# Two GCN layers with graph attention on one core: seeding products in PSUM, another form of the layer norm, another order of steps

## The chip, the cores and the metric

The kernel runs on one core of a Trainium2 chip. The metric is the time of one execution on the device, in microseconds (us). The engines are called as in the profile: PE (TensorE, matrix products), DVE (VectorE), ACT (ScalarE), POOL (GpSimd) and SP (SyncE, which here only issues DMAs).

## The reference

64 graphs of 256 nodes with 512 features pass through two layers, all in float32. The first is a three-layer graph convolution, the second an attention that is restricted to sums over neighbours; each is added to its input and normalized over the features.

```
def _gcn_layer(x, adj, W, b):
    return adj @ (x @ W) + b

# layer 0
h = relu(_gcn_layer(x, adj, W1, b1)); h = relu(_gcn_layer(h, adj, W2, b2))
x = layernorm(x + _gcn_layer(h, adj, W3, b3))
# layer 1
q, k = split(x @ Wqk);  v = x @ Wv
agg = adj @ (k * mask)
w = mask * sum(q * agg, axis=-1) / sqrt(512)
x = layernorm(x + softmax(w, axis=nodes)[:, :, None] * v)
```

layernorm is (x - mean)/sqrt(var + 1e-5), without a gain or an offset. x has the shape (64, 256, 512) and adj (64, 256, 256); the adjacency is symmetric in its pattern only, so it comes transposed as an input of its own.

## The kernel before, in words

**Tiling.** Two graphs make a pair, and there are 32 pairs. A pair's nodes are two blocks of 128 (on the partitions) and the features two halves of 256. An operation on such a quarter of both graphs is 128x512: one PSUM bank.

**Products by Strassen.** Every product of 2 x 2 blocks is done with seven block products in place of eight (Winograd's form). `seven` (line 104) runs them in the order P1, P7, P6, P2, P5, P4, P3 on three PSUM banks: x takes P1, and then P6, P5 and P3 are added onto it; v takes P7 and then P4; y takes P2. Between them the other engines take out intermediate results: t1 (P1), u (x after P6) and t7 (P7) are copied to an SBUF tile `tmp` by ACT (line 109), or, where a matrix is to be added ("plus"), by an add on DVE (line 111). The four blocks of the result are c11 = y + t1, c22 = x + t7, c21 = v + u and c12 = x. PSUM has 8 banks in one pool (line 41). [...]

**Block sums.** The sums and differences of blocks that Strassen needs are made by `unit` (line 61). It puts an operation on DVE if its name is in `ON_DVE` (line 35), and on POOL otherwise. Names are made of a stage and a sum: "c1T7" is sum T7 of the first support product, "h17" and "x5" are sums of the moving matrix, "a3" and "a7" sums of the adjacency, "b3" the addition of the bias b3 to x.

**Stages of one pair.** Each is a Python generator that issues one block product, or one small group of operations, and yields:
- F, `front` (line 407): support product c1 (X W1, line 290), aggregation h1 (adj times it with relu, line 331), c2, h2, and c3; `load_xT` of the next pair after c1, and `load_x` (line 81) after h2.
- S, `sums` (line 417): the block sums of the next pair's x, the four b3 additions to this pair's x, and the adjacency sums of the next pair.
- B, `back` (line 433): layer 3's aggregation with x as plus (line 367), statistics, `inv_std` (line 371), the layer norm's `apply` (line 459), 32x32 transposes of the normalized r into `tr` on DVE (line 488), and from `tr` by DMA through `via` in DRAM into x1T (lines 491 to 495). `apply` does two things for each of four 128x512 parts: ACT writes the masked and scaled copy xm from r (line 460), and then DVE normalizes r in place (line 462).
- G, `gather`: adj times xm, which gives agg's factor, kept in gt.
- M, `attention` (line 515): Z and I are block sums of x1T for a nested Strassen; then come 7 + 7 products for a and b, taken in turn, and 7 + 7 for c and d (line 546), whose weights stream through a ring of 7 buffers. c and d have as plus the sums of R that DVE makes at lines 580 to 584 between the two. `score` (line 563) multiplies with gt and sums.
- E, `finish` (line 594): softmax over the nodes, v times the weights plus r, layer norm, and the output DMA.

**Order.** In round i the generators run for different pairs: F and S for pair i, B, G and M for pair i-1, and E for pair i-2. `run` (line 633) takes them in the order of a string in which each letter is one step: START for round 0, ORDER for rounds 1 to 30, LAST for round 31, and END for the last layers of pair 31. The schedule is manual: each engine has the instructions of its queue in the order in which the steps issue them, and the framework adds only the semaphore waits. So a letter's place in the string sets the place of all its instructions on PE, DVE, ACT, POOL and SP.

**Buffers.** tmp has 5 buffers, the support blocks (`sup`) 9; r is read by the layer norm, by the transposes and by E of the next round; x and xm share one buffer by tag, and so do tr and gt, and x1T and R's second part.

Of the kernel before, what the change touches and what calls it, by code (L numbers as in the profile page):

```python
# [9 lines left out]
FP = mybir.dt.float32  # L10
AF = mybir.ActivationFunctionType
OP = mybir.AluOpType
AX = mybir.AxisListType

P = 128
# [5 lines left out]
def gcn_then_graph_attention(ctx: ExitStack, tc: tile.TileContext, xT, xN, adjT, mask, W1, b1, W2, b2, W3, b3,  # L21
# [9 lines left out]
    KEYS = ("T1", "T2", "T3", "T4")  # L31
    SUP = 9
    SBUFS = 6
    TMP = 5
    ON_DVE = ('a5', 'c2T5', 'c2T6', 'c3T6', 'c3T7', 'h13', 'h23', 'h27', 'x3', 'x5')

    const = ctx.enter_context(tc.tile_pool(name="const", bufs=1))
    pool = ctx.enter_context(tc.tile_pool(name="work", bufs=1))
    small = ctx.enter_context(tc.tile_pool(name="small", bufs=2))
    dram = ctx.enter_context(tc.tile_pool(name="dram", bufs=2, space=bass.MemoryType.DRAM))  # L40
    psum = ctx.enter_context(tc.tile_pool(name="psum", bufs=8, space=bass.MemoryType.PSUM))

    E = mybir.EngineType
    ctx.enter_context(tc.manual_schedule(engines={E.PE, E.DVE, E.Activation, E.Pool, E.SP}))

    def bank(shape=(P, G, N)):
        return psum.tile(list(shape), FP, name="ps", tag="ps")

    def tmp():
        return pool.tile([P, D], FP, name="tmp", bufs=TMP)  # L50
# [53 lines left out]
    def seven(mm, shape, c11, c12, c21, c22, plus=None):  # L104

        def out(ps, k):
            t = shaped(shape)
            if plus is None:
                nc.scalar.copy(t, ps)  # L109
            else:  # L110
                add(t, ps, plus[k])
            return t

        x = bank(shape)
        mm(1, x, True)
        t1 = out(x, 0)
        yield
        v = bank(shape)
        mm(7, v, True)
        yield  # L120
        mm(6, x, False)
        u = out(x, 1)
        yield
        y = bank(shape)
        mm(2, y, True)
        t7 = out(v, 2)
        c11(y, t1)
        yield
        mm(5, x, False)
        c22(x, t7)  # L130
        yield
        mm(4, v, False)
        c21(v, u)
        yield
        mm(3, x, False)
        c12(x)
        yield
# [25 lines left out]
    def warm(n):  # L163

        ps = bank((P, P))
        for _ in range(n):
            nc.tensor.matmul(ps, lhsT=ident, rhs=ident, start=True, stop=True)

    warm(10)
    wl = {}  # L170
    begin, end = load_w(W1, 1, True)
# [110 lines left out]
    def support(src, w, who, last=None):  # L282

        sup = lambda: pool.tile([P, G, HD], FP, name="sup", tag="sup", bufs=SUP)
        C = {k: sup() for k in (3, 1, 5, 7, 6)}

        def mm(n, ps, first):
            for g in range(G):
                for c in range(2):
                    nc.tensor.matmul(ps[:, g], lhsT=src[n][:, c, g], rhs=w[n][:, c],  # L290
                                     start=(first and g == 0 and c == 0), stop=(g == G - 1 and c == 1),
                                     skip_group_check=True)

        def c21(v, t):
            add(C[5], v, t)
            unit(who + "T7", C[7], C[3], C[5], OP.subtract)
            unit(who + "T6", C[6], C[7], C[1])

        def c12(x):
            C[2], C[4] = sup(), sup()  # L300
            nc.scalar.copy(C[2], x)  # L301
            unit(who + "T5", C[5], C[5], C[1], OP.subtract)
            sub(C[4], x, C[6])
        steps = seven(mm, (P, G, HD), lambda y, t: add(C[3], y, t), c12, c21, lambda v, t: add(C[1], v, t))
        for _ in range(2):
            next(steps)
            yield
        if last is not None:
            last()
        yield from steps  # L310
        return C

    def aggregate(C, aS, b, who):

        hT = [pool.tile([P, 2, G, N], FP, name="hT", tag="act", bufs=2) for _ in range(2)]
        src, first, rest, last = a_sums(blocks(hT), who)
        blk = blocks(hT)

        def relu(i, j, ps=None):
            o = blk(i, j)  # L320
            for c in range(2):
                nc.scalar.activation(o[:, c], (o if ps is None else ps)[:, c], AF.Relu, bias=b[:, 2 - 2 * j + c:3 - 2 * j + c])  # L322

        def block(i, j, a, t):
            add(blk(i, j), a, t)
            relu(i, j)

        def mm(n, ps, first):
            for c in range(2):
                for g in range(G):  # L330
                    nc.tensor.matmul(ps[:, c, g], lhsT=C[n][:, g, c * P:(c + 1) * P], rhs=aS[n][:, g],  # L331
                                     start=(first and c == 0 and g == 0), stop=(c == 1 and g == G - 1),
                                     skip_group_check=True)
        for k, _ in enumerate(seven(mm, (P, 2, G, P), lambda y, t: block(0, 0, y, t), lambda x: relu(0, 1, x),
                                    lambda v, t: block(1, 0, v, t), lambda v, t: block(1, 1, v, t))):
            if k == 5:
                first()
            if k == 6:
                rest()
            yield  # L340
        return src, last
# [29 lines left out]
    def inv_std(mvt, n=G):  # L371

        sd = small.tile([P, NH, n], FP, name="sd")
        nc.scalar.activation(sd, mvt[:, :, :, 1], AF.Sqrt, bias=eps)  # L374
        rs = small.tile([P, NH, n], FP, name="rs")
        nc.vector.reciprocal(rs, sd)  # L376
        nb = small.tile([P, NH, n], FP, name="nb")
        nc.vector.scalar_tensor_tensor(nb, mvt[:, :, :, 0], -1.0, rs, op0=OP.mult, op1=OP.mult)  # L378
        return rs, nb

    def softmax_rows(w, gs):

# [50 lines left out]
    def back(i, C, aS, x, mask_t, end, put):  # L433
# [13 lines left out]
        yield from adj_times(aS, C, lambda y, t: add(rb(0, 1), y, t), lambda x: block(rb(0, 0), x, xb(0, 0), 0),  # L447
                             lambda v, t: block(rb(1, 1), v, t, 1), lambda v, t: add(rb(1, 0), v, t),
                             plus=(xb(0, 1), xb(1, 1), xb(1, 0)))

        rs, nb = inv_std(mvt)
        yield
        mrs = small.tile([P, NH, G], FP, name="mrs")
        nc.vector.scalar_tensor_tensor(mrs, rs, ISCALE, mask_t, op0=OP.mult, op1=OP.mult)
        mnb = small.tile([P, NH, G], FP, name="mnb")
        nc.vector.scalar_tensor_tensor(mnb, nb, ISCALE, mask_t, op0=OP.mult, op1=OP.mult)
        xm = pool.tile([P, G, NH, D], FP, name="xm", tag="x", bufs=1)

        def apply(h, g):
            nc.scalar.activation(xm[:, g, h, :], r[:, g, h, :], AF.Identity, scale=mrs[:, h, g:g + 1],  # L460
                                 bias=mnb[:, h, g:g + 1])
            nc.vector.tensor_scalar(r[:, g, h, :], r[:, g, h, :], rs[:, h, g:g + 1], nb[:, h, g:g + 1],
                                    op0=OP.mult, op1=OP.add)
        hg = [(h, g) for h in range(NH) for g in range(G)]
        xmb = [[xm[:, :, h, j * HD:(j + 1) * HD] for j in range(2)] for h in range(2)]
        if end:
# [1 line left out]
            x1T = [pool.tile([P, 2, G, N], FP, name="x1T", tag="act", bufs=2) for _ in range(2)]  # L468
            x1b = lambda h, k: x1T[k][:, :, :, h * P:(h + 1) * P]
            for h, g in hg:  # L470
                apply(h, g)
            yield
            xS = t_sums(xmb)
            for h, g in hg:
# [6 lines left out]
        else:  # L481
# [1 line left out]
            x1T = pool.tile([P, P, NH, 2, 2, G], FP, name="x1T", bufs=1)  # L483
            x1b = lambda h, k: x1T[:, :, h, k].rearrange("p n c g -> p c g n")
            for h, g in hg:
                apply(h, g)
# [13 lines left out]
        gb = lambda h, j: gt[:, h, :, j * HD:(j + 1) * HD]  # L500

        def gather():
            steps = adj_times(aS, xS, lambda y, t: add(gb(0, 0), y, t), lambda x: nc.scalar.copy(gb(0, 1), x),
                              lambda v, t: add(gb(1, 0), v, t), lambda v, t: add(gb(1, 1), v, t))
# [10 lines left out]
    def attention(i, x1b, w, r, mask_t, put):  # L515
# [23 lines left out]
        def inner(q, R, more=None):  # L539
# [15 lines left out]
            return seven(mm, (P, len(outer), HD), lambda y, t: add(R[:, :, 0, 0], y, t), c12,  # L555
                         lambda v, t: add(R[:, :, 1, 0], v, t), lambda v, t: add(R[:, :, 1, 1], v, t), plus=plus)
        v = pool.tile([P, G, NH, D], FP, name="v", tag="v", bufs=1)
        flat = lambda R: R.rearrange("p g j f -> p g (j f)")
# [35 lines left out]
    def finish(i, prev, gs=range(G)):  # L594
# [20 lines left out]
        rs, nb = inv_std(mvt, n)  # L615
        yield
        for k, g in enumerate(gs):
            for h in range(NH):
# [2 lines left out]
                yield  # L621
            nc.sync.dma_start(out[i, :, g * NH * D:(g + 1) * NH * D].rearrange("p (h f) -> p h f", h=NH), v[:, g])

    ORDER = ("BBFEFFBEBFBFBFBFFFBEFFFFBFSFBBBFFFBBBFGFFGGFFGFEEGMFFGMMMEGMMSFFMEMMEMMEFESMMEEFFMSM"
             "SMMMFMMMMFFEMMMMMMMMSMMMMMMFSMMMSSMMSSM")
    START = ("FFFBFBBFFBFBBBBBFFFFFFBBBBBFBBBBBBBBBBBFFBBBBSBFFBSBFBBFFFBBFBBFBFSFBFFBBBBFBBSFFBSB"
             "BSFBSFFSBBBSBBBBBSFBBBBBSBSBB")
    LAST = ("FBBSEFBFEBBFFBFBFBFFBFFFFEBBFFBBFBFBEFEEGFEGGFFEGEFFMMGSFFGMMMMFEFMMMMEMMMMMMEMMMFMM"
            "GSMMMMEMMMMMMMMFMMMSSMMMFMSSSFMFFSFSFSM")
    END = ("BEBBBBBBEBBBBBBBBGMGMEMMBEGGEEMGEGEMMMMMMEMEEMEMMMMMMMMMMMGMMBMMMMMMMMMMXMMXXMMMXYXM"  # L630
           "XMYXYMYYMYXYMYXYBMYMMXXYYXM")

    def run(order, rest, **gens):
        res = {}
# [81 lines left out]
```

## Time and profile before

| | |
|---|---|
| median of three runs | 2762.42 us (2761.38 to 2765.03) |
| the profiled execution | 2765.32 us |
| its span | 2763.5 us |
| mean granted clock of PE | 0.996 |
| busy in the span | PE 98%, PE's weight loads 87%, DVE 78%, ACT 41%, POOL 46% |
| matmuls' records, all | 14290 |
| DMA moved | 403.71 MB, mean 146 GB/s |

The page gives for each group of instructions its line, engine, operation, and out<-in by the names of the program, the count, the busy time, the mean of one in ns, and the idle time of its engine before it with what ended it. In the timeline, a line is a run of like instructions: its start in us, its length, engine, line, operation, tiles and count, and in brackets the wait ahead of it and its releaser. PEld stands for weight loads, SPq for issues of SP's queue. The ends of matmuls are modelled, so a stage on PE is best measured from start to start.

### The profile page before, as it was taken

What the parts mean: (1) busy time and instruction counts of PE and PEld (TensorE: products, weight loads), DVE (VectorE), ACT (ScalarE), POOL (GpSimd) and SP (SyncE); (2) the same over time, 40 slices, a digit from 0 to 9 for tenths busy, and PEclk for the clock granted to TensorE, in tenths of its full rate; (3) what the DMA queues carried; (4) which work ended last, traced back from release to release, by engine and by line L of the source; (5) the groups of instructions that cost most, each with busy time, mean ns of one, the idle gap of its engine ahead of it and who ended that gap; (6) DMA issues with size and microseconds to landing.
All of it is one profiled execution on the core that took longest, in us unless ns stands there. A gap on an engine that the chain in (4) does not pass through costs nothing. (4 is left out here: it accounts for less than half of the span.)

```text
span 2763.5 us, 41007 instructions
## 1 busy us (share of the span) xinstructions
PE 2716.9 (98%) x14290; PEld 2401.7 (87%) x14290; DVE 2145.0 (78%) x3828; ACT 1133.1 (41%) x2050; POOL 1262.8 (46%) x966
## 2 busy tenths in 40 slices
PE   9999999999999999999999999999999999999996
PEld 8888888888888888888888888888888888888885
DVE  5778777877777777778777777877787877778777
ACT  3434344434344343443334443434433444434343
POOL 3535455444554354544445543445544455434442
PEclk9999999999999999999999999999999999999998
DMA  6534554344544445543455444455434554434553
GB/s 209 165 110 147 165 175 135 117 143 154 163 151 123 126 147 162 173 135 112 143 162 162 141 129 131 147 162 176 133 115 141 161 162 148 130 123 147 162 155 97
DMA packets 202233, 403.71 MB, mean 146 GB/s; under 512 B 24752, under 2 KB 61872, under 8 KB 193968
## 3 DMA queue, kind: packets, MB, share of 16 engines
q1 hardware_dynamic: 202032, 401.10, 46.5%
q8 instruction: 117, 1.92, 0.3%
q14 instruction: 84, 0.69, 0.1%
HBM read 328.54 MB, written 72.48 MB: 145 GB/s over the span
## 5 line engine op out<-in xcount | busy, mean ns | idle before, releaser
L109 ACT COPY tmp<-ps 128x512 f32<-128x512 f32 x768 | 431.3, 584 | 643.3 <-PE ps L290 257.1
L62 POOL TENSOR_TENSOR sup<-sup 128x512 f32<-128x512 f32 x160 | 218.1, 1372 | 565.9 <-DVE sup L53 409.2
L546 PE MATMUL ps<-ring,I 128*128 128x256 f32 x1792 | 433.0, 381 | 7.7 <-DVE tmp L53 3.0
L546 PEld LDWEIGHTS ps<-ring,I 128*128 128x128 f32 x1792 | 334.1, 190 | 66.3 <-DVE R L53 11.7
L290 PE MATMUL ps<-w_T,S 128*128 128x256 f32 x1536 | 351.0, 381 | 9.2 <-POOL S L62 7.6
L301 ACT COPY sup<-ps 128x512 f32<-128x512 f32 x96 | 56.2, 586 | 722.2 <-PE ps L290 722.2
L290 PEld LDWEIGHTS ps<-w_T,S 128*128 128x128 f32 x1536 | 286.7, 190 | 59.7 <-POOL S L62 20.5
L546 PE MATMUL ps<-ring,Z 128*128 128x256 f32 x1344 | 327.9, 380 | 1.1 <-ACT Z L524 1.1
L59 POOL TENSOR_TENSOR I<-Z 128x384 f32<-128x384 f32 (+1 forms) x128 | 190.1, 1504 | 244.5 <-DVE Z L527 150.8
L546 PEld LDWEIGHTS ps<-ring,Z 128*128 128x128 f32 x1344 | 254.4, 190 | 38.4 <-ACT Z L524 3.3
L331 PEld LDWEIGHTS ps<-aT,sup 128*128 128x128 f32 x2048 | 253.5, 192 | 13.2 <-issue 6.6
L331 PE MATMUL ps<-aT,sup 128*128 128x128 f32 x2048 | 261.8, 276 | 1.8
L53 DVE TENSOR_TENSOR R<-ps,tmp 128x512 f32<-128x512 f32 (+1 forms) x384 | 221.2, 616 | 48.7 <-PE ps L546 48.4
L62 POOL TENSOR_TENSOR x<-x,b3b 128x512 f32<-128x512 f32 x128 | 192.2, 1523 | 128.7 <-DMA x<-in_xN 119.3
L290 PE MATMUL ps<-w,hT 128*128 128x256 f32 x1024 | 242.0, 379 | 0.0
L290 PE MATMUL ps<-w_T,hT 128*128 128x256 f32 x1024 | 236.5, 379 | 0.0
L290 PEld LDWEIGHTS ps<-w_T,hT 128*128 128x128 f32 x1024 | 194.6, 190 | 26.5
L53 DVE TENSOR_TENSOR sup<-ps,tmp 128x512 f32<-128x512 f32 x288 | 192.8, 677 | 30.8 <-PE ps L290 30.7
L290 PEld LDWEIGHTS ps<-w,hT 128*128 128x128 f32 x1024 | 192.0, 190 | 24.7
L331 PE MATMUL ps<-aS,sup 128*128 128x128 f32 x1536 | 206.3, 279 | 1.7 <-ACT tmp L109 1.1
L322 ACT ACTIVATE hT<-hT,b 128x256 f32<-128x256 f32 x384 | 167.4, 501 | 87.1 <-DVE hT L53 86.2
L331 PEld LDWEIGHTS ps<-aS,sup 128*128 128x128 f32 x1536 | 188.9, 192 | 11.4 <-DVE hT L53 4.8
(116 smaller groups left out, 4762.8 us busy)
## 6 DMA issues: line engine op xcount, KB each, us to landing
ring<-mv SPq DMA_DIRECT2D x672, 256.0 KB, 3.6
x<-in_xN SPq DMA_DIRECT2D x32, 1024.0 KB, 8.0
out<-v SPq DMA_DIRECT2D x64, 512.0 KB, 7.6
xT<-in_xT SPq DMA_DIRECT2D x31, 1024.0 KB, 5.0
via<-tr SPq DMA_DIRECT2D x31, 1024.0 KB, 4.2
x1T<-via SPq DMA_DIRECT2D x124, 256.0 KB, 4.7
ring<-mv SPq DMA_DIRECT2D x224, 128.0 KB, 3.1
aT<-in_adjT SPq DMA_DIRECT2D x32, 512.0 KB, 3.9
```

Source lines behind the costliest of these rows:

```text
L53: nc.vector.tensor_tensor(o, a, b, op=OP.add)
L59: (nc.gpsimd).tensor_tensor(o, a, b, op=op)
L62: (nc.vector if name in ON_DVE else nc.gpsimd).tensor_tensor(o, a, b, op=op)
L109: nc.scalar.copy(t, ps)
L290: nc.tensor.matmul(ps[:, g], lhsT=src[n][:, c, g], rhs=w[n][:, c], start=(first and g == 0 and c == 0), stop=(g == G - 1 and c == 1), skip ...
L301: nc.scalar.copy(C[2], x)
L322: nc.scalar.activation(o[:, c], (o if ps is None else ps)[:, c], AF.Relu, bias=b[:, 2 - 2 * j + c:3 - 2 * j + c])
L331: nc.tensor.matmul(ps[:, c, g], lhsT=C[n][:, g, c * P:(c + 1) * P], rhs=aS[n][:, g], start=(first and c == 0 and g == 0), stop=(c == 1 and ...
L546: nc.tensor.matmul(ps[:, k], lhsT=left[n](place[o]), rhs=wt[:, k], start=(first and k == 0), stop=(k == len(outer) - 1), skip_group_check= ...
```

## The change

What it does, in parts:

1. *Seeds.* In `seven`, P1's result is copied by ACT (or added to its plus by DVE) straight into the bank y, in PSUM, instead of into an SBUF tmp. P2 is then accumulated onto it with `start` false. c11 therefore is y alone: an ACT copy to its place, or in `aggregate` a relu that reads y, in place of a DVE add of y and t1. y comes from a pool of its own of two banks; the other pool has six. At the start of the program 16 small matmuls with an identity write both seed banks.
2. *Layer norm of layer 0.* `turn`, on DVE and first, is (r - mean)*rs in place. `masked`, on ACT and after it, is xm = r*ms, with ms = mask/sqrt(512). Before it was ACT first, from the raw r with a scale and an offset, and then DVE. The small tiles nb, mrs and mnb go in `back` (nb stays in `finish`); ms is new.
3. *Engines of the sums.* `ON_DVE` gains a3, a6, a7, b3, c1T5, c1T6, c1T7, c2T7, h17, h25 and h26, and loses c3T6, h13, x3 and x5.
4. *Order.* All four strings are new.

```diff
-    ON_DVE = ('a5', 'c2T5', 'c2T6', 'c3T6', 'c3T7', 'h13', 'h23', 'h27', 'x3', 'x5')
+    SEEDS = 2
+    ON_DVE = ('a3', 'a5', 'a6', 'a7', 'b3', 'c1T5', 'c1T6', 'c1T7', 'c2T5', 'c2T6', 'c2T7', 'c3T7', 'h17', 'h23', 'h25', 'h26', 'h27')
-    psum = ctx.enter_context(tc.tile_pool(name="psum", bufs=8, space=bass.MemoryType.PSUM))
+    psum = ctx.enter_context(tc.tile_pool(name="psum", bufs=8 - SEEDS, space=bass.MemoryType.PSUM))
+    def seed_bank(shape=(P, G, N)):
+        return psum.tile(list(shape), FP, name="seed", tag="seed", bufs=SEEDS)
...
         x = bank(shape)
         mm(1, x, True)
-        t1 = out(x, 0)
+        y = seed_bank(shape)
+        if plus is None:
+            nc.scalar.copy(y, x)
+        else:
+            add(y, x, plus[0])
         yield
...
-        y = bank(shape)
-        mm(2, y, True)
+        mm(2, y, False)
         t7 = out(v, 2)
-        c11(y, t1)
+        c11(y)
...
+    seeds = [seed_bank((P, 4, P)) for _ in range(SEEDS)]
+    for t in seeds:
+        for k in range(4):
+            nc.tensor.matmul(t[:, k], lhsT=ident, rhs=ident, start=(k == 0), stop=(k == 3), skip_group_check=True)
     warm(10)
...
-        steps = seven(mm, (P, G, HD), lambda y, t: add(C[3], y, t), c12, c21, lambda v, t: add(C[1], v, t))
+        steps = seven(mm, (P, G, HD), lambda y: nc.scalar.copy(C[3], y), c12, c21, lambda v, t: add(C[1], v, t))
...
-        for k, _ in enumerate(seven(mm, (P, 2, G, P), lambda y, t: block(0, 0, y, t), lambda x: relu(0, 1, x),
+        for k, _ in enumerate(seven(mm, (P, 2, G, P), lambda y: relu(0, 0, y), lambda x: relu(0, 1, x),
...
-        rs, nb = inv_std(mvt)
-        yield
-        mrs = small.tile([P, NH, G], FP, name="mrs")
-        nc.vector.scalar_tensor_tensor(mrs, rs, ISCALE, mask_t, op0=OP.mult, op1=OP.mult)
-        mnb = small.tile([P, NH, G], FP, name="mnb")
-        nc.vector.scalar_tensor_tensor(mnb, nb, ISCALE, mask_t, op0=OP.mult, op1=OP.mult)
+        ms = small.tile([P, NH, G], FP, name="ms")
+        nc.vector.tensor_scalar(ms, mask_t, ISCALE, None, op0=OP.mult)
+        rs = inv_std(mvt)
+        yield
...
-        def apply(h, g):
-            nc.scalar.activation(xm[:, g, h, :], r[:, g, h, :], AF.Identity, scale=mrs[:, h, g:g + 1],
-                                 bias=mnb[:, h, g:g + 1])
-            nc.vector.tensor_scalar(r[:, g, h, :], r[:, g, h, :], rs[:, h, g:g + 1], nb[:, h, g:g + 1],
-                                    op0=OP.mult, op1=OP.add)
+        def turn(h, g):
+            nc.vector.tensor_scalar(r[:, g, h, :], r[:, g, h, :], mvt[:, h, g, 0:1], rs[:, h, g:g + 1],
+                                    op0=OP.subtract, op1=OP.mult)
+
+        def masked(h, g):
+            nc.scalar.activation(xm[:, g, h, :], r[:, g, h, :], AF.Identity, scale=ms[:, h, g:g + 1])
...
-    ORDER = ("BBFEFFBEBFBFBFBFFFBEFFFFBFSFBBBFFFBBBFGFFGGFFGFEEGMFFGMMMEGMMSFFMEMMEMMEFESMMEEFFMSM"
-             "SMMMFMMMMFFEMMMMMMMMSMMMMMMFSMMMSSMMSSM")
+    ORDER = ("BBFEFFBBEFBBFBFBFFFFFBFFFFBFBBBFFFBFSEBGGFSGGEFEEGFMSGMFMGMFMFMFMMMEMMFMFMMMSMFEEESM"
+             "SMEMFEFSEFMMMFMSMMMMSMMMMMMMMSMMMMSMMMF")
```

The products c11 of `back` (layer 3), of G and of M change in the same way as that of `support`: each add of y and t becomes an ACT copy of y. In ORDER, counted by letters: c3's last product moves to the very end of the round; the steps of S come at letters 36 to 118 in place of 26 to 121, the x sums (36, 42, 52) ahead of most of M; of b3's four steps (76, 82, 84, 91) three stand ahead of the sums of R (lines 580 to 584; letters 85, 87 and 94), and in before two (82, 84; sums at 87, 89, 90), there on POOL. The first part of the layer norm is issued after P2 of h1 (before: after P4), the second after P1 of c2, the third and fourth after P7 of c2 (before: three after P1 of c2).

More of the change, by code (lines that the diff above doesn't have):

```diff
@@ L376, in inv_std @@
         nc.vector.reciprocal(rs, sd)
-        nb = small.tile([P, NH, n], FP, name="nb")
-        nc.vector.scalar_tensor_tensor(nb, mvt[:, :, :, 0], -1.0, rs, op0=OP.mult, op1=OP.mult)
-        return rs, nb
+        return rs
     def softmax_rows(w, gs):
@@ L446, in block @@
                     nc.vector.bn_aggr(mvt[:, h, g], st[:, h, g])
-        yield from adj_times(aS, C, lambda y, t: add(rb(0, 1), y, t), lambda x: block(rb(0, 0), x, xb(0, 0), 0),
+        yield from adj_times(aS, C, lambda y: nc.scalar.copy(rb(0, 1), y), lambda x: block(rb(0, 0), x, xb(0, 0), 0),
                              lambda v, t: block(rb(1, 1), v, t, 1), lambda v, t: add(rb(1, 0), v, t),
                              plus=(xb(0, 1), xb(1, 1), xb(1, 0)))
-        rs, nb = inv_std(mvt)
+        ms = small.tile([P, NH, G], FP, name="ms")
+        nc.vector.tensor_scalar(ms, mask_t, ISCALE, None, op0=OP.mult)
+        rs = inv_std(mvt)
         yield
-        mrs = small.tile([P, NH, G], FP, name="mrs")
-        nc.vector.scalar_tensor_tensor(mrs, rs, ISCALE, mask_t, op0=OP.mult, op1=OP.mult)
-        mnb = small.tile([P, NH, G], FP, name="mnb")
-        nc.vector.scalar_tensor_tensor(mnb, nb, ISCALE, mask_t, op0=OP.mult, op1=OP.mult)
         xm = pool.tile([P, G, NH, D], FP, name="xm", tag="x", bufs=1)
-        def apply(h, g):
-            nc.scalar.activation(xm[:, g, h, :], r[:, g, h, :], AF.Identity, scale=mrs[:, h, g:g + 1],
-                                 bias=mnb[:, h, g:g + 1])
-            nc.vector.tensor_scalar(r[:, g, h, :], r[:, g, h, :], rs[:, h, g:g + 1], nb[:, h, g:g + 1],
-                                    op0=OP.mult, op1=OP.add)
+        def turn(h, g):
[3 more added lines that the diff above has]
+            nc.scalar.activation(xm[:, g, h, :], r[:, g, h, :], AF.Identity, scale=ms[:, h, g:g + 1])
         hg = [(h, g) for h in range(NH) for g in range(G)]
@@ L470, in back @@
             for h, g in hg:
-                apply(h, g)
+                turn(h, g)
+                masked(h, g)
             yield
@@ L485, in back @@
             for h, g in hg:
-                apply(h, g)
+                turn(h, g)
+                masked(h, g)
                 for k in range(2):
@@ L502, in gather @@
         def gather():
-            steps = adj_times(aS, xS, lambda y, t: add(gb(0, 0), y, t), lambda x: nc.scalar.copy(gb(0, 1), x),
+            steps = adj_times(aS, xS, lambda y: nc.scalar.copy(gb(0, 0), y), lambda x: nc.scalar.copy(gb(0, 1), x),
                               lambda v, t: add(gb(1, 0), v, t), lambda v, t: add(gb(1, 1), v, t))
@@ L554, in inner @@
                 plus = (more[:, :, 0, 0], more[:, :, 1, 0], more[:, :, 1, 1])
-            return seven(mm, (P, len(outer), HD), lambda y, t: add(R[:, :, 0, 0], y, t), c12,
+            return seven(mm, (P, len(outer), HD), lambda y: nc.scalar.copy(R[:, :, 0, 0], y), c12,
                          lambda v, t: add(R[:, :, 1, 0], v, t), lambda v, t: add(R[:, :, 1, 1], v, t), plus=plus)
@@ L614, in finish @@
                 nc.vector.bn_aggr(mvt[:, h, k], st[:, h, k])
-        rs, nb = inv_std(mvt, n)
+        rs = inv_std(mvt, n)
+        nb = small.tile([P, NH, n], FP, name="nb")
+        nc.vector.scalar_tensor_tensor(nb, mvt[:, :, :, 0], -1.0, rs, op0=OP.mult, op1=OP.mult)
         yield
@@ L622, in finish @@
             nc.sync.dma_start(out[i, :, g * NH * D:(g + 1) * NH * D].rearrange("p (h f) -> p h f", h=NH), v[:, g])
-    ORDER = ("BBFEFFBEBFBFBFBFFFBEFFFFBFSFBBBFFFBBBFGFFGGFFGFEEGMFFGMMMEGMMSFFMEMMEMMEFESMMEEFFMSM"
-             "SMMMFMMMMFFEMMMMMMMMSMMMMMMFSMMMSSMMSSM")
[L626 to L631, printed above, removed]
+    ORDER = ("BBFEFFBBEFBBFBFBFFFFFBFFFFBFBBBFFFBFSEBGGFSGGEFEEGFMSGMFMGMFMFMFMMMEMMFMFMMMSMFEEESM"
+             "SMEMFEFSEFMMMFMSMMMMSMMMMMMMMSMMMMSMMMF")
+    START = ("BBFFFFFBBFFBBBBBFFFFFFFBBBBBFSFBBBBSBBBFBBBBBFBBBBBBBFBBFFFFFFBSFFFFSBBBBBBFSFBFBSBS"
+             "BBFBBSFSSBSBBBBBBBBBBBFBBBSBB")
+    LAST = ("FFBEBFBBEBBFFBSFBFFFEFFBSFSFFBFBFFBBFBBEEFGEEEGFGGFGFMMFMGFMFMFGMFMEEMMMMFMFFMMMSSEM"
+            "SMSFMSEMMFSFMMMMMEMFMMMMMMMMMMFMMSMMMSM")
+    END = ("BBBBBBBBBBBEBBBBGGEMGGMEMBGEEEBGMMMMEMMMMEMEMMEEEBMMMMMMGMMMMMMMMMMMMMMMMXMMXXMMXYMX"
+           "YMYXMXMXYXYMMXMMYYYYXYYMXMY")
     def run(order, rest, **gens):
```

## The prediction

> **What bounds the kernel now.** I read part 1 of the page first, then the start of each round (one round is one pair) in the timeline, then one middle round, 1005.35 to 1090.76, line by line in the timeline, and last the groups by form and the waits.
>
> ```profile
> PE 2716.9 (98%) x14290; PEld 2401.7 (87%) x14290; DVE 2145.0 (78%) x3828; ACT 1133.1 (41%) x2050; POOL 1262.8 (46%) x966
> ```
>
> ```profile
> 76.75 1.89 PE L290 MATMUL ps<-w,xT 128*128 128x256 f32 x8
> 2523.56 1.89 PE L290 MATMUL ps<-w,xT 128*128 128x256 f32 x8
> ```
>
> TensorE is the bound. From the first product of c1 in one round to that in round 30 lie (2523.56 - 76.75)/29 = 84.37 us each. What PE must do in a round: the trace records two instructions for a matmul, issued 0.216 us apart for 256 columns (8 in 1.73) and 0.112 us for 128. A round has 322 x 0.216 = 69.5, 112 x 0.112 = 12.5 and some 0.4 of softmax: 82.4. So 84.37 - 82.4 = about 1.9 us of each round is PE standing still, and only that can be won. The other engines have slack: per round DVE 67, POOL 39.5, ACT 35.4 busy. What matters is where PE stands still. The timeline of the middle round:
>
> ```profile
> 1021.19 3.85 POOL L62 TENSOR_TENSOR sup<-sup 128x512 f32<-128x512 f32 x3 [12.48 <-DVE sup L53]
> 1022.42 1.05 PE L331 MATMUL ps<-aT,sup 128*128 128x128 f32 x8
> 1023.31 2.12 PE L331 MATMUL ps<-aS,sup 128*128 128x128 f32 x16
> 1025.27 3.14 PE L331 MATMUL ps<-aT,sup 128*128 128x128 f32 x24
> 1028.37 1.16 PE L331 MATMUL ps<-aS,sup 128*128 128x128 f32 x8
> 1029.36 1.89 PE L290 MATMUL ps<-w,hT 128*128 128x256 f32 x8
> 1030.15 1.27 POOL L62 TENSOR_TENSOR S<-hT 128x512 f32<-128x512 f32 x1 [5.12 <-ACT hT L322]
> 1031.48 3.72 PE L290 MATMUL ps<-w_T,S 128*128 128x256 f32 x16 [0.23 <-POOL S L62]
> 1031.87 2.23 ACT L460 ACTIVATE xm<-r,mnb,mrs 128x512 f32<-128x512 f32 x3
> 1032.72 1.65 DVE L462 TENSOR_SCALAR r<-r,rs,nb 128x512 f32<-128x512 f32 x1
> 1035.32 0.47 DVE L462 TENSOR_SCALAR r<-r,rs,nb 128x512 f32<-128x512 f32 x1
> 1036.74 0.47 DVE L462 TENSOR_SCALAR r<-r,rs,nb 128x512 f32<-128x512 f32 x1
> ```
>
> Three readings. First, h1 takes 1029.36 - 1022.42 = 6.94 for 56 products worth 6.27: 0.67 lost, behind POOL's three c1 operations T7, T6, T5 at 1.28 each. Second, c2 starts at 1029.36 and its P7 at 1031.48, 2.12 where 1.73 is due: with 0.11 behind it, 0.50 lost for h17, one POOL operation of 1.27. Third, the same in-place operation of line 462 costs 0.47, or 1.65 [...].
>
> ```profile
> 1071.99 5.68 POOL L62 TENSOR_TENSOR x<-x,b3b 128x512 f32<-128x512 f32 x3 [4.29 <-DMA x<-in_xN]
> 1081.15 1.46 PE L546 MATMUL ps<-ring,Z 128*128 128x256 f32 x6
> 1082.25 1.61 DVE L53 TENSOR_TENSOR tmp<-ps,R 128x512 f32<-128x512 f32 x3
> 1082.99 1.56 PE L546 MATMUL ps<-ring,I 128*128 128x256 f32 x6 [0.38 <-DVE tmp L53]
> 1084.39 1.46 PE L546 MATMUL ps<-ring,Z 128*128 128x256 f32 x6
> ```
>
> Fourth: in the c and d products PE waits for DVE's adds of "more" (tmp), 0.96 us in this round. Start of M: 0.59. Softmax: 0.24. Sum: 2.96. The next round loses only 1.45: c1/h1, h17 and softmax recur, the rest varies (mean of c/d about 0.4).
>
> ```profile
> L109 ACT COPY tmp<-ps 128x512 f32<-128x512 f32 x768 | 431.3, 584 | 643.3 <-PE ps L290 257.1 <-DVE r L53 152.4 <-PE ps L367 135.5
> L53 DVE TENSOR_TENSOR R<-ps,tmp 128x512 f32<-128x512 f32 x288 | 192.0, 683 | 48.7 <-PE ps L546 48.4
> L462 DVE TENSOR_SCALAR r<-r,rs,nb 128x512 f32<-128x512 f32 x128 | 109.8, 858 | 49.8 <-ACT xm L460 49.8
> ```
>
> [...]
>
> **The change part by part.** Each cost is per round.
>
> *Seeds.* A round has eleven runs of `seven`; three have a plus (layer 3's product, here L3, and c and d). DVE loses c11 where ACT copies now: c1, c2, c3, G, a, b are 6 x 0.68; h1 and h2 lose an add and relu reads PSUM, 2 x 0.68; L3, c and d lose 0.69 + 0.68 + 0.42. Together 7.2. ACT gains 9 copies of about 0.58, less in d: about 5. The seed itself is the old copy with another goal: [...] I take 0.584. PE's count stays; 16 matmuls at the start lie under the load of W1, which PE awaits until 9.5. Is there a new wait of PE? P2 now waits for the seed. But P6, which goes into the bank of P1, already waited for that same reader, and P2 comes after P6: no. Two banks of eight are set aside; each seven holds three at a time, and the seed bank turns over once in two sevens, 5 us or more for a reader of 0.6: nil. If that cover goes, it is one ACT copy, 0.6.
>
> *ON_DVE.* To DVE: a3, a6, a7, b3 (four), c1T5 to T7, c2T7, h17, h25, h26, at about 0.65 (0.35 for the a's): 8.9. To POOL: c3T6, h13, x3, x5 twice: -4. Layer norm loses small DVE operations, -0.45. DVE: 67 - 7.2 - 0.45 + 8.9 - 4 = about 64 of 84; ACT 40; POOL 28. No engine becomes the bound by its sum.
>
> *c1 to h1.* Three operations of 0.65 in place of 1.28 and c11 gone from DVE ahead of them: 0.67 falls to about 0.2. Next late is the ACT relu chain. Gain 0.47.
>
> *h17.* 0.66 for 1.27 (0.61 sooner), but it queues behind h1's last add on DVE: 0.50 to about 0.25. Gain 0.25.
>
> *c and d.* DVE loses 1.1 of c11 here and gets the four b3 adds. These wait for x (issued at the start of c3, landing 8.0 later by the table of DMA issues; the shortest I found was 6.9) and hold DVE's queue: the sum of R parts, 1.23 each, and the adds of "more" stand behind. From landing to P6 of c DVE needs 3 x 0.65 (b3) + 2 x 1.23 + 3 x 0.65 + 1.22 + 0.65 + 0.36, which ends some 0.3 to 0.6 before P6 of c is due. With that slack the stall goes from 0.4 to 0.05, gain 0.35. If x lands at its latest (8.8) [...], P6 of c is 0.4 to 1.0 late.
>
> *Layer norm.* In before ACT reads r first and DVE waits for it; now `turn` goes first, the transposes start 0.8 sooner, and `masked` waits for `turn`. Queued behind the masked ones on ACT is the copy of P6 of c2, for which P5 of c2 waits. From the end T of h17: turns start at T, T + 1.43 and T + 2.85 (cycle by the two last lines of line 462: 1036.74 - 1035.32 = 1.42, a turn and two transposes). Then 0.47 + 0.81 + 0.58 and semaphores: T + 4.8. P5 is due at T + 3 x 1.73 = T + 5.2: slack 0.35. POOL runs h16, h15, h13 at that time[...]. New wait, taken at 0; its ends are 0 and 2.0.
>
> *Order.* More DVE work beside POOL in G's third product and in h2: -0.15. Start of M, where the Z copies queue on ACT behind more copies: -0.1. Softmax keeps 0.24. Ends for both: 0 and twice that.
>
> Sum: 0.47 + 0.25 + 0.35 - 0.25 = 0.82 a round. 30 rounds: -25. The last layer norm, with nothing to hide it, hands r on about 1.3 sooner, and some finish work moves: -2. The profiled execution was 2765.3 (span 2763.5 and 1.8 around it), 2.9 above the median of 2762.4: 2765.3 - 27 = 2738, against the median 2736 to 2738; I say 2737, 0.9% faster.
>
> **The rivals.** *More gained:* all waits but softmax and 0.25 more go, as the next round with its 1.45 shows that c/d and M's start may be nil. 1.9 - 0.5 = 1.4 x 30 + 2 = 44: 2718. For it: DVE's load falls just where PE waited. Against it: the two new waits in the queues. *Given back:* x late [...], +0.8: 0.82 goes to 0, 2763. [...] *Slower:* [...] P5 of c2 waits 2.0 behind `masked` on ACT. In nine rounds of ten that is 1.8 on the mean: +1.8 - 0.82 = +1.0, x 30 less 2 = 28: 2790. In every round, with the adds of c 0.5 late as well, it would be +1.7 and 2811. It decides from where the fourth turn ends later than T + 3.65 by more than 0.8. [...] *Not what it says:* the seed adds no product and removes none, so if all stalls were set by DMA nothing would change; the three recurring stalls name POOL and DVE, so I leave it within the given-back case.
>
> **How the numbers follow.** Forecast 2737: 0.48. More gained, 2718: 0.18. Given back, 2763: 0.12. Slower, 2790: 0.22. What a measurement of this kernel can tell from no change is about 0.2%, 5.5 us; so faster 0.66, same 0.12, slower 0.22. Range: from 2714, just under the bigger gain (leaving under 0.05), to 2780, which cuts most of the slower case (0.15). Forecast and bigger gain have their own range, 2714 to 2750.
>
> **What would show it.** Right: rounds of 83.5 us from c1 to c1; h1 in under 6.5; P7 of c2 within 1.9 of its start; no PE wait at P6 of c; the tmp copies of line 109 down from 768 to 512 and 256 new ACT copies into the seed bank at some 0.58. Wrong: PE waits at line 290 for an ACT tmp in c2, turns of 1.65 more often than one in four, PE waiting for DVE's tmp at the first adds of c just behind x's landing, or seeds much over 0.66. The prediction is wrong altogether if a round is 84.4 or more.

## Result and profile after

The kernel after took 2727.74 us (median of four runs, 2725.27 to 2730.18), the kernel before 2763.73 in the same measurement (2761.38 to 2769.49). The ratio is 0.9864, with a 95% interval of 0.9846 to 0.9882: 36 us or 1.4% faster. The forecast was 2737. The direction held; 36 us were gained where the prediction had summed 27.

Page of after, part 1, the line that answers to the one shown of before:

```profile
PE 2694.6 (99%) x14306; PEld 2410.4 (89%) x14306; DVE 2118.6 (78%) x3700; ACT 1278.4 (47%) x2338; POOL 925.5 (34%) x678
```

PE has 16 more records and 99% of the span. These are the start-up matmuls with the identity: 8 of them (two banks by four), with two records each, so "16 matmuls" in the part on the change and in the prediction counts records. ACT took 145 us more, 4.5 a round (5 was the estimate), POOL 337 less. DVE has hardly less to do, 2119 for 2145.

Start of rounds 1 and 30, timeline of after:

```profile
78.21 1.89 PE L301 MATMUL ps<-w,xT 128*128 128x256 f32 x8
2487.96 1.89 PE L301 MATMUL ps<-w,xT 128*128 128x256 f32 x8
```

(2487.96 - 78.21)/29 = 83.09 us a round, where before had 84.37. Most rounds of after are 83.03 to the hundredth: 82.43 of products and 0.60 of standing still. The 1.28 per round are 37.1 us in 29 rounds. The work from the start of round 31 to the last product is 3.35 shorter, round 30 is 1.1 shorter, and the first round (round 0) ends 1.5 later: 40 us in all, the difference of the two spans (2763.5 and 2723.5). The medians lie 36 apart, since the profiled execution of after was the fastest of its four.

The seams around h1 and c2, timeline of after, one round that starts at 992.01 (line numbers of after: 342 is aggregation, 301 support, 467 `turn`, 471 `masked`, 113 the tmp copy):

```profile
1009.08 1.05 PE L342 MATMUL ps<-aT,sup 128*128 128x128 f32 x8
1015.69 1.89 PE L301 MATMUL ps<-w,hT 128*128 128x256 f32 x8
1016.44 0.69 DVE L66 TENSOR_TENSOR S<-hT 128x512 f32<-128x512 f32 x1 [0.97 <-ACT hT L333]
1017.42 3.62 PE L301 MATMUL ps<-w_T,S 128*128 128x256 f32 x16
1019.98 0.46 DVE L467 TENSOR_SCALAR r<-r,mvt,rs 128x512 f32<-128x512 f32 x1
1020.47 0.72 ACT L471 ACTIVATE xm<-r,ms 128x512 f32<-128x512 f32 x1 [0.70 <-DVE r L467]
1021.10 1.05 ACT L113 COPY tmp<-ps 128x512 f32<-128x512 f32 x2
```

h1 takes 1015.69 - 1009.08 = 6.61 (6.94 before, 6.27 due; the prediction's sign was under 6.5). P7 of c2 starts 1.73 after c2, with no wait, and h17 is done 0.3 before. The fourth turn costs 0.46. None of the 128 turns is longer than 0.6, where in before 31 of 128 took over 1.4. POOL was running beside all of those 31. But it also ran beside 62 turns of after, and beside the third turn of 31 rounds of before, and each of these took under 0.5: POOL at work does not by itself make the operation long here. `masked` waits 0.70 for it, and the copy of u for c2's P5 is behind `masked`, as foreseen; P5 doesn't wait.

The start of the c products, same round:

```profile
1055.14 1.90 DVE L66 TENSOR_TENSOR x<-x,b3b 128x512 f32<-128x512 f32 x3 [2.08 <-DMA x<-in_xN]
1062.81 1.02 DVE L57 TENSOR_TENSOR seed<-ps,R 128x512 f32<-128x512 f32 x2
1063.82 2.54 PE L556 MATMUL ps<-ring,I 128*128 128x256 f32 x11
```

DVE stands 2.08 us waiting for x with the b3 adds, and the seeds of c and d are there in time all the same: PE runs 11 instructions without a gap. One line more from the groups by form, and one from the page's table of DMA issues:

```profile
L122 ACT COPY seed<-ps 128x512 f32<-128x512 f32 x256 | 146.1, 571 | 307.9 <-PE ps L301 167.4 <-PE ps L378 112.2 <-PE ps L342 19.0
```

```profile
x<-in_xN SPq DMA_DIRECT2D x32, 1024.0 KB, 5.2
```

A seed costs ACT 571 ns (584 for a copy to tmp in before), and the copies to tmp are down from 768 to 512, as the signs said. x lands in 5.2 us, where before had 8.0; in the new order the output's two DMAs are issued 6.3 and 8.2 us behind x, not 1.4 and 4.3.

Where PE stood still, in us per round. For this table I took the start-to-start times of PE's instructions, less 0.216 (256 columns) or 0.112 (128), where more than 0.03 was left, and added them by stage over rounds 1 to 29:

| | c1 end, h1 | P7 of c2 | start of M | c, d | softmax | round |
|---|---|---|---|---|---|---|
| before | 0.67 | 0.49 | 0.06 | 0.46 | 0.23 | 84.37 |
| after | 0.36 | 0 | 0 | 0.06 | 0.23 | 83.09 |

### The profile page after: what moved, and what is told of

Read it like the earlier page. It is cut to its first block, busy times and chain, and to the rows that moved or that the text cites. A ratio compares the mean times of both kernels' runs of the same rounds, so it can differ in the third digit from the quotient of the medians.

```text
span 2723.5 us, 41056 instructions
## 1 busy us (share of the span) xinstructions
PE 2694.6 (99%) x14306; PEld 2410.4 (89%) x14306; DVE 2118.6 (78%) x3700; ACT 1278.4 (47%) x2338; POOL 925.5 (34%) x678
## 5 line engine op out<-in xcount | busy, mean ns | idle before, releaser
L66 POOL TENSOR_TENSOR S<-hT,S 128x512 f32<-128x512 f32 x64 | 93.1, 1454 | 1005.3 <-DVE S L66 1005.3
L113 ACT COPY tmp<-ps 128x512 f32<-128x512 f32 x512 | 287.2, 588 | 123.3 <-PE ps L301 60.9
L122 ACT COPY seed<-ps 128x512 f32<-128x512 f32 x256 | 146.1, 571 | 307.9 <-PE ps L301 167.4
L66 POOL TENSOR_TENSOR sup<-sup 128x512 f32<-128x512 f32 x64 | 81.8, 1298 | 589.3 <-DVE sup L66 589.3
L66 DVE TENSOR_TENSOR sup<-sup 128x512 f32<-128x512 f32 x224 | 219.5, 981 | 10.3 <-DVE sup L57 0.5
L556 PE MATMUL ps<-ring,Z 128*128 128x256 f32 x896 | 219.5, 379 | 0.0
L57 DVE TENSOR_TENSOR R<-ps,tmp 128x512 f32<-128x512 f32 (+1 forms) x256 | 153.4, 621 | 74.2 <-PE ps L556 65.9
L556 PEld LDWEIGHTS ps<-ring,Z 128*128 128x128 f32 x896 | 167.7, 190 | 21.8 <-DVE tmp L57 0.4
L301 PE MATMUL ps<-w,S 128*128 128x256 f32 x768 | 182.8, 381 | 2.5 <-DVE sup L57 2.5
L565 ACT COPY R<-seed 128x512 f32<-128x512 f32 (+1 forms) x128 | 66.5, 545 | 242.0 <-PE seed L556 242.0
```

The source lines that it names most:

```text
L57: nc.vector.tensor_tensor(o, a, b, op=OP.add)
L66: (nc.vector if name in ON_DVE else nc.gpsimd).tensor_tensor(o, a, b, op=op)
L122: nc.scalar.copy(y, x)
L556: nc.tensor.matmul(ps[:, k], lhsT=left[n](place[o]), rhs=wt[:, k], start=(first and k == 0), stop=(k == len(outer) - 1), skip_group_check= ...
L565: return seven(mm, (P, len(outer), HD), lambda y: nc.scalar.copy(R[:, :, 0, 0], y), c12, lambda v, t: add(R[:, :, 1, 0], v, t), lambda v, ...
```

## Experiments

The ratio is always to the kernel before on the same chip in the same measurement, with its 95% interval; after is 0.9864. The first theory was that of the prediction, parts that add up: the sums moved to DVE take away the waits of h1 and c2, seeds clear DVE for c and d. The rivals put the whole gain in the seeds, or in the order. Four runs undo one part of after each; three put one part alone, or one sum of a part, into before. Then come runs for the single terms.

**One E letter moved** (needed for the next run). Without seeds c11 of layer 3 is a DVE add into r. In the new order it stands on DVE ahead of `finish`, which must first read the r of the pair before, on DVE too: each would wait for the other. So this run and the next move E ahead by one letter.

```diff
-    ORDER = ("BBFEFFBBEF...
+    ORDER = ("BBFEFFBEBF...
-    LAST = ("FFBEBFBBEBB...
+    LAST = ("FFBEBFBEBBB...
```

> The kernel after, with one E letter (the second step of finish) moved one letter ahead, in front of the fourth product of layer 3, in ORDER and LAST; nothing else. It is the partner of the run without seeds, which needs that place. All theories: within 0.1% of after, some 2728, since PE's own queue changes by two small matmuls' place only.

Measured: 2748.15, 0.9934 (0.9921 to 0.9946). All expectations missed: one letter costs 0.7% of the 1.4%. Timeline of this run, round from 997.55 (line 613 is v*s + r of `finish`):

```profile
1004.81 2.74 DVE L613 SCALAR_TENSOR_TENSOR v<-v,s,r 128x512 f32<-128x512 f32 x4
1007.46 0.68 DVE L57 TENSOR_TENSOR tmp<-ps,x 128x512 f32<-128x512 f32 x1
1008.20 1.13 PE L378 MATMUL ps<-sup,aT 128*128 128x256 f32 x4 [0.33 <-DVE tmp L57]
```

Four DVE operations of 2.74 us stand ahead of layer 3's t7, and PE waits for it, 0.57 a round in the table's measure. Only the seed allows the faster place: with c11 on ACT, the write to r waits on ACT's queue (4.5 us in after) and DVE can take t7 first.

**Without seeds.**

```diff
-        y = seed_bank(shape)
-        if plus is None:
-            nc.scalar.copy(y, x)
-        else:
-            add(y, x, plus[0])
+        t1 = out(x, 0)
...
-        mm(2, y, False)
-        c11(y)
+        y = bank(shape)
+        mm(2, y, True)
+        c11(y, t1)
```

> After without seeds: P1 goes to a tmp again, P2 starts its own bank, c11 is a DVE add of both (relu behind it in h1 and h2); one pool of 8 banks; the same E letter moved as in the partner. Layer norm, engines of the sums and order stay. Theory (the sums moved to DVE took the waits away, seeds only clear DVE a little): 7.2 us more on DVE per round cost some 0.3 in c and d and 0.1 in h1, about 12 us in all, 2740. Rival (the seeds are the gain, as without them DVE can't carry the moved sums): DVE at about 73 of 83 us per round falls behind at c1/h1, h17 and c/d, 1.0 or more per round, 2758 or more.

Measured: 2788.81, 1.0083 (1.0070 to 1.0096). Against its partner that is 41 us, 1.13 a round (84.907 for 83.774): the rival's size, not the theory's. But it isn't lost at all the seams that the rival named. P7 of c2 and c/d keep their gain. Nearly all of it is one place, the last product of h1, which stands still 1.35 a round where its partner stands 0.22; P7 of h1 loses another 0.23, and other places give a little back. Timeline:

```profile
1035.94 1.26 DVE L53 TENSOR_TENSOR hT<-ps,tmp 128x512 f32<-128x512 f32 x2
1036.67 1.16 PE L331 MATMUL ps<-aS,sup 128*128 128x128 f32 x8 [1.09 <-DVE hT L53]
```

With c11's add ahead of it on DVE, the first part of the layer norm (turn and two transposes, to 1036.09) is still on DVE when c22's add is due, and P3, which uses that bank, waits.

**The old order in after.** All four strings as in before.

> After with the four order strings of before; seeds, layer norm and engines of the sums stay. Theory (engines of the sums): h17 and c1/h1 keep their gain of 0.8 per round, c and d lose it, as x lands in 8 us beside the output again and the b3 adds on DVE wait for it in front of the sums of R: 0.4 to 1.0 per round, 2740 to 2758. Rival (order is the gain): nearly all comes back, 2758 or more, with the 0.5 wait for h17 there too.

Measured: 2855.63, 1.0327 (1.0313 to 1.0341). Far beyond both expectations: worse than before by 89 us. Per round: start of M 1.46, P6 of c3 0.85 and P6 of c2 0.63, both released by an ACT seed copy by the profile, h1 0.6, a later product of M 0.27. P7 of c2 keeps its gain, and so do c and d (0.02), although the theory expected them to lose it; h1 keeps little.

**The old division of sums in after.** ON_DVE as in before.

> After with the ON_DVE of before; seeds, layer norm and order stay. Theory (engines of the sums): h17 on POOL again costs its 0.49 per round, c1's T7 to T5 on POOL 0.3 more in h1, 30 rounds of 0.8: 2752. Rival (seeds): 2735 or less, since c11 is gone from DVE either way. Rival (order): 2735 or less.

Measured: 2831.85, 1.0236 (1.0221 to 1.0251). Missed by 80 us. The theory's two places are there, P7 of c2 with 0.48 and h1 with 1.2; but P3 of G, its last product, loses 1.3, and the start of M 0.5. P3 goes on 0.05 after DVE's add into gt ends, in every round. That add is late by DVE's own queue: its sum c2T6 waits for c2T7, which is POOL's again, 2.8 us in each round (89.9 in 32), and in the round read DVE worked almost without a gap from there to the add.

With this the theory of adding parts was given up. Theory now: order, division of the sums, seeds and layer norm are one setting. Each sets where instructions stand in the engines' queues, and a change of one without the others shows waits that neither kernel has. The expectations from here on name it "theory now".

**The old layer norm in after.** `apply` for `turn` and `masked`.

> After with the layer norm of before (ACT writes xm from the raw r first, DVE normalizes in place behind it, with nb, mrs and mnb); seeds, engines of the sums and order stay. First theory of parts that add up: within 5 us of after, 2733 or less. Theory now (each part is needed by the order string[...]): the first part stands in h1, and its ACT copy comes only behind the relus of c11, so DVE waits for it some 2 us in front of the adds of h1's last blocks, and PE with it: 1.5 to 2.2 per round, 2772 to 2795.

Measured: 2830.2, 1.0241 (1.0226 to 1.0256): theory now by mechanism and place, but 35 us above its range. Timeline (473 is the in-place part, 471 ACT's):

```profile
1049.91 0.83 ACT L471 ACTIVATE xm<-r,mnb,mrs 128x512 f32<-128x512 f32 x1
1050.78 0.55 DVE L473 TENSOR_SCALAR r<-r,rs,nb 128x512 f32<-128x512 f32 x1 [2.60 <-ACT xm L471]
1052.97 1.30 PE L342 MATMUL ps<-aS,sup 128*128 128x128 f32 x8 [2.05 <-DVE hT L57]
1054.07 3.47 PE L301 MATMUL ps<-w,hT 128*128 128x256 f32 x8
```

DVE waits 2.60 for ACT, and h1's last product 2.2 behind that. The last line is the part that wasn't foreseen: the next product begins at 1057.37, 3.30 after c2's first and not 1.73 (see the end). The start of M loses 0.64 besides.

**Seeds alone, in before.**

> Before with seeds alone; its layer norm, engines of the sums and order stay. First theory (parts add up, seeds relieve DVE by 7.2 per round): c and d lose their 0.4 of waits and h1 0.1 to 0.2, some 15 us faster than before, ratio 0.994. Theory now (order and queues must fit): ACT has the seed copies of c2 and c3 behind other ACT work of the old order, and P6, which uses the bank that the copy reads, waits for them 0.5 to 1.5 per round: ratio 1.000 to 1.010.

Measured: 2805.73, 1.0155 (1.0141 to 1.0169). Slower, as theory now had it, but not for its reason: P6 of c2 and c3 show no new wait. More than all of the 1.30 a round is 1.46 at the third product of M; c and d still wait 0.36. The profile names POOL's I as releaser, whose needed part was done long before. By the kernel's text that product (P7 of a) opens a new bank, and DVE's add into gt is the last to read the bank of G's v. If the product takes over that bank, it waits for this add: six banks turn over sooner than eight. The next run tests it.

**The banks alone, in before.** Two for y, six for the rest; no seeds.

```diff
-    psum = ... bufs=8 ...
+    SEEDS = 2
+    psum = ... bufs=8 - SEEDS ...
...
-        y = bank(shape)
+        y = seed_bank(shape)
```

> Before with only the banks divided as in after: y comes from a pool of two banks, all else from six in place of eight. No seeds, no other change. Theory (what seeds alone lost at the start of M is the bank: the third product of M takes the bank that DVE's add into gt must give back, where eight banks had another free): the same 1.4 per round as with seeds alone, and c/d as in before, ratio 1.015. Rival (POOL's sum I, which the profile names as releaser, is late through the ACT copies of the seeds): 1.000.

Measured: 2845.62, 1.0289 (1.0275 to 1.0303). It is the division of the banks, and more than expected. Timeline:

```profile
1081.91 0.68 DVE L57 TENSOR_TENSOR gt<-ps,tmp 128x512 f32<-128x512 f32 x1
1081.99 1.28 POOL L63 TENSOR_TENSOR I<-I,Z 128x512 f32<-128x512 f32 x1
1082.69 1.10 PE L550 MATMUL ps<-ring,I 128*128 128x256 f32 x4 [1.85 <-POOL I L63]
```

PE goes on 0.10 after DVE's add into gt ends (1082.59), and it does so in all 31 rounds, in the run with seeds alone and in that with the old order as well. The POOL sum that starts at 1081.99 is still running, and the one before it ended 0.77 ahead of PE here and 0.17 in those two runs, so POOL isn't what PE waited for. The profile doesn't show which bank the product takes; the fixed 0.10 and this run speak for the one that DVE reads. The start of M costs 2.1 a round, c and d 0.9. In the old order, then, dividing the banks costs 86.86 - 84.37 = 2.49 a round, and the seeds give back 86.86 - 85.67 = 1.19 of it.

**h17 alone on DVE, in before.**

> Before with h17 alone moved from POOL to DVE. Prediction's step: 0.25 per round gained, 7.5 us, ratio 0.9973. If the whole wait of 0.49 goes, as in after: 14.6 us, ratio 0.9947. Rival (DVE's queue has the in-place part of the layer norm, which waits for ACT, ahead of it): nothing or a loss, ratio 1.000 or more.

Measured: 2784.78, 1.0079 (1.0066 to 1.0092): the rival's side. Timeline (109 is the tmp copy, 53 DVE's add):

```profile
1038.42 1.97 PE L290 MATMUL ps<-w_T,S 128*128 128x256 f32 x8 [0.21 <-ACT tmp L109]
...
1046.89 1.35 PE L290 MATMUL ps<-w,S 128*128 128x256 f32 x5 [0.46 <-DVE sup L53]
```

P7's 0.49 goes indeed. But P6 now comes earlier and waits 0.45 for the copy of P1's bank, which stands on ACT behind xm and the relus (line 109; its idle time is put down at 0.21); and with DVE's part of the layer norm later, c2's last product waits 0.73 for c22's add. One wait of 0.49 became two of 1.18.

**h17 alone back on POOL, in after.**

> After with h17 alone back on POOL. Theory (the wait is POOL's 1.27 against DVE's 0.66, whole): 0.45 to 0.6 per round back, 13 to 18 us more than after, ratio 0.991 to 0.993. Prediction's step: 0.25 per round, ratio 0.989. Rival (in the new order other things hide it): 0.9865 as after.

Measured: 2746.27, 0.9929 (0.9917 to 0.9942): the whole wait. P7 of c2 loses 0.48, c and d 0.14, round 83.73. One more thing comes back: the third turn of a round takes 1.16 in 31 rounds, where in after no turn is longer than 0.6. P5 of c2 doesn't wait for that (c2 is 0.5 later here as well). The same step is worth a gain of 0.64 a round in after and a loss of 0.68 (85.05 - 84.37) in before.

**The new order alone, in before** (with the E letter moved).

> Before with the four order strings of after alone (one E letter moved ahead as in the first run, since without seeds DVE's write into r would stand in front of E's read of the same buffer). Theory of the order as the gain [...]: ratio 0.990 or less. Theory now (order fits only its own engines): h17, c1's sums and the layer norm stand late in their queues, 1.0 to 3.0 per round more, ratio 1.010 to 1.035.

Measured: 3052.57, 1.1044 (1.1023 to 1.1064). Slower as theory now had it, by three times its size: round 93.33, with h1's last product waiting 3.2, h1's others 1.4, G 2.6; 0.57 is the moved letter's. The granted clock was 0.979 to 0.986 here, where before had 0.995 to 0.997 in the same measurement, so part of it is the slower instructions of the last section. The order is no gain by itself.

**x three products later, in after.** `load_x` becomes a step of its own, L, behind one product of c3 and two of M.

```diff
-        put["x"], put["mask"] = load_x(i)
...
+            gens["L"] = late_x(i, put)
...
-    ORDER = "...MMFMFMMMSMFEEES...
+    ORDER = "...MMFMFMMLMSMFEEES...
```

> After with the load of x issued one product of c3 and two of M later (about 3.4 us) in the middle rounds; it then meets the output, as in before, so that x is there about 4 us later. Nothing else moves. Prediction's step (b3 on DVE waits for x ahead of the sums of R, slack 0.3 to 0.6 from a landing at 8.0, x now landing 0.6 to 1.5 behind that): 0.3 to 1.2 per round, 9 to 36 us more, ratio 0.990 to 1.000. If the wait has its full effect with little slack, as DVE already waits 1.2 for x in after: 2 to 3.5 per round, ratio 1.008 to 1.025. Rival (b3 has slack in plenty): 0.9865.

Measured: 2791.17, 1.0093 (1.0079 to 1.0106), round 85.35, 2.26 more. Timeline:

```profile
1082.52 1.90 DVE L66 TENSOR_TENSOR x<-x,b3b 128x512 f32<-128x512 f32 x3 [6.02 <-DMA x<-in_xN]
...
1089.66 1.02 DVE L57 TENSOR_TENSOR seed<-ps,R 128x512 f32<-128x512 f32 x2
1090.46 1.53 PE L559 MATMUL ps<-ring,I 128*128 128x256 f32 x6 [1.74 <-issue]
```

The size is that of the full effect with little slack. The chain that the prediction drew, x to b3 to R's sums to the seeds to P6 of c, is there. DVE waits 173.4 us for x in 30 rounds, in after 37.0 in 31: 4.6 a round more. PE loses 2.3 of it, so the slack of after is about 2.3.

**The fourth masked copy twice, in after.**

```diff
                 masked(h, g)
+                if (h, g) == hg[-1]:
+                    masked(h, g)
```

> After with the fourth masked copy on ACT done twice (0.73 more on ACT ahead of the copy of c2's P6; the result is the same). Prediction's step (slack 0.35 at P5 of c2): 0.4 per round lost, 12 us, ratio 0.991. From after's trace (slack about 0.9): 0 to 0.1 per round, ratio 0.9865 to 0.9875.

Measured: 2729.48, 0.9869 (0.9855 to 0.9882). P5 of c2 waits 0.055 in every round. Of 0.73 more on ACT 0.67 were slack.

## Why the prediction was right, and where its sum was off

*What bounds the kernel* held: 82.4 of products per round (82.43 in after), the standing still of PE as all that can be won, and the places where it stood. The other engines' sums played no part. They have two slips that cancel: at its own prices the sums that go to DVE are 8.2 (11 of 0.65 and 3 of 0.35), not 8.9, and those that leave it are five operations, 3.3, not 4. DVE came to 66 a round, not 64.

| step, us per round | forecast | measured |
|---|---|---|
| c1 to h1 | +0.47 | +0.31 |
| h17 | +0.25 | +0.49 |
| c and d | +0.35 | +0.40 |
| layer norm, new wait | 0 | 0 |
| order, start of M | -0.25 | +0.06 |
| sum | 0.82 | 1.26 |

*c1 to h1* was too large by 0.16, and most of what came of it has another cause than the step gave. It put the whole 0.67 down to POOL's three sums. In before only the 0.17 ahead of P6 stands behind these. 0.22 is h1's last product, which waits for c22's add from the bank (it has 0.2 too little behind P4); that is the same in both kernels. And 0.29 is P5, which waits for ACT's copy of u. Timeline of before, the round of the prediction:

```profile
1025.47 0.30 ACT L374 ACTIVATE sd<-mvt,eps 128x4 f32<-128x4 f32 x1
1025.67 1.05 ACT L109 COPY tmp<-ps 128x512 f32<-128x512 f32 x2
```

Line 374 is the square root of the layer norm's statistics. It stands just ahead of the copy in ACT's queue, behind a table load of 1.28, and P5 goes on 0.14 after the copy, in every round. In after the root stands ahead of h1 (at 1008.30 in the round shown). The run with the old order and the moved sums tells the two apart: there P6 waits 0.09, but P5 still 0.30. So the moved sums gave about 0.08 of the gain, and the order about 0.24, a term that the prediction has only as a loss.

*h17* was mis-sized by half. I charged DVE with a queue ahead of it. In after DVE stands idle 0.97 in front of h17, waiting for relu, so the shorter operation counts in full. The run with h17 on POOL gives the same 0.48.

*c and d* came out nearly as forecast, but that is luck as far as the runs show. Which part of the change did it stays open: of the parts undone none brings the 0.46 back (0.05 without seeds, 0.02 with the old order, 0.16 with the old sums, 0.19 with the old layer norm), so DVE's relief by the seeds, which the step named, isn't needed; and seeds alone in before leave 0.36. One figure was wrong besides: the step took x's landing of 8.0 from before, though the new order moves the output's DMAs off x. It is 5.2. By the slack of 2.3 measured above, I estimate that 8.0 (2.8 later) would have cost about 0.5 a round. That is worked out, not run.

*Layer norm.* The rival that ends slower, P5 of c2 behind `masked`, didn't come; its 2.0 was an estimate, from two turns a round of 1.65 in place of 0.47. The slack is 0.67 where I had 0.35: P7 of c2 begins 0.29 after h17 ends, not with it, and a masked copy takes 0.72, not 0.81. No turn took longer than 0.6. That h17 has left POOL is part of the reason: with h17 back there one turn in four takes 1.16. What else makes a turn long was not shown. What the step missed is how much `turn` first matters in this order: with ACT first PE loses 2.1 more in h1 alone. I costed the form of the layer norm only by its tail.

*Order* was the worst term: 0.25 lost was expected, and nothing is. I had taken the new strings as a shuffle whose cost is some contention, and the moved sums for the gain. The runs show that neither stands without the other: in before the order alone costs 9 us a round, in after the old order costs 3.7 and the old sums 3.3.

*Seeds.* "No new wait of PE" and "nil" for the banks hold in after, but not in the old order. In the old order the six banks cost 2.5 a round, and with the other parts of after in it P6 waits for the seed copy, 0.63 and 0.85. The cover that I priced at one ACT copy of 0.6 was far larger, and I had not named it: the place of G's last adds ahead of M. That a bank needs the start-up matmuls ahead of its first seed was my assumption, and no run with seeds leaves them out. They cost nothing that lasts, as forecast: P1 of the first c1 begins at 8.12 for 5.92, but P2 already at 13.30 for 13.65.

*The end* gained 3.35, where 2 was forecast.

What stays open: how the gain divides among the parts, that of c and d above all. Each of the four parts undone takes back more than all of it (61 to 128 us, without the seeds 41 beyond the moved letter), and all those done alone lose. So the question has no answer in numbers that add up. The new form of the layer norm alone, and all moved sums alone, were not run.

## What to carry to other kernels

Where a kernel runs on fixed queues at 98% of its bound engine, cost a bundle of edits as one setting: walk the new order with the new durations, queue by queue, since a part alone says nothing of its worth within the bundle (h17 on DVE: 0.68 lost in one, 0.64 gained in the other). An edit that moves a write from one engine to another can be worth much for the order it allows: the one letter that only the seeds permit is 0.68 of the 1.28 a round. And before an engine is named as releaser, see in every round how long before the wait's end its operation ended: the wait that came with the divided banks, 2.1 us a round, showed here under another name, while the add that PE waited for ended 0.10 ahead of it in every round of three runs.

## What the runs showed of the hardware

In three runs TensorE's granted clock was down behind some of PE's waits. In the run with the old layer norm PE stood 2.2 us longer than due in each round. Windows of its timeline from 1048 on (columns: span, busy time of PE, PEld, DVE, ACT and POOL, then the granted clock):

```profile
1048.00:1054.00 6.00, 3.95 (x34) 3.76 (x33) 2.88 (x8) 3.57 (x8) 0.00 (x0) 0.99 0.00 0
1054.00:1058.00 4.00, 4.00 (x13) 3.29 (x12) 0.69 (x1) 1.80 (x5) 2.48 (x3) 0.59 0.00 0
```

In the four us behind the wait the clock is 0.59, and eight instructions take 3.30 from start to start, 0.41 apart where 0.216 was due: about 1.6 us lost on top. In rounds 1 to 30 that happened after 10 of 30 such waits (mean clock of the execution 0.990, in after 0.996). In the run with x later it happened after 4 of 7 waits of 2.2 to 2.9 (mean 0.993), and in the run with the order alone after 13 of 30 waits of 3.0 (0.979). It did not happen after the waits of 1.5 to 2.0, 29 in the run with the banks alone (0.996) and 13 in that with x later, nor after a single one of 2.35 with the banks alone. In after's trace the clock was 0.50 from 2672.7 to 2676.1 as well, with no wait of PE over 0.64 in the six us ahead. In the round shown, then, a wait of 2.2 and the slow stretch behind it cost 3.8 together. What decides between the 10 and the other 20 was not shown; by these counts it isn't the length alone.

ACT's write into PSUM (571 ns, mean of 256) was 2 to 3% shorter than into SBUF (588 in the same run, 584 in before). That is too small to matter here.
